# A Perceiver layer on one core: small tensor work of cross attention in two groups instead of three, and a new order of opening, loads and stores

## The chip, the cores and the metric

The kernel runs on one core of a Trainium2 chip. TensorE (PE) multiplies matrices, VectorE (DVE), ScalarE (ACT) and GpSimd (POOL) do elementwise work, and each engine works off its own queue of instructions in order. Transfers are issued from a queue too: nearly all of them here from SyncE's (SP). The metric is the device time of one execution in microseconds. Three executions of the kernel before are given, with their median; one more was taken with the hardware profiler.

## The reference

One layer of a Perceiver block with 16 batches: 64 latents of 512 numbers attend to 512 context rows of 512 numbers and to themselves (8 heads of 64), then the 1,024 latent rows attend to each other within a batch by differential self attention, then a gated feed-forward net follows whose weights and inputs are rounded to a 4-bit float format in blocks of 16. Cut to what matters, for each batch:

```python
# cross attention; g_*, b_* are layer norm vectors
latents = layer_norm(x)
xn, ln = layer_norm(ctx, g_x, b_x), layer_norm(latents, g_l, b_l)
q      = ln @ w_q                             # 64 x 512, 8 heads of 64
k, v   = split(concat([xn, ln]) @ w_kv, 2)    # 576 x 512 each
sim    = q @ k.T * 64**-0.5                   # masked by the context mask
x      = x + layer_norm(softmax(sim) @ v @ w_out, g_o, b_o)
# self attention: two softmax maps a head, their difference weighs v, then Wo
x      = x + diff_attention(layer_norm(x), Wq, Wk, Wv, Wo)
# feed forward: fp4 rounds to the 4-bit grid, a scale for each block of 16
z      = fp4(layer_norm(x))
h      = silu(z @ fp4(w_gate).T) * (z @ fp4(w_up).T)
x      = x + fp4(h) @ fp4(w_down).T
```

## The kernel before

Everything is worked in fp32r products of split numbers: each operand is a high part (a cast) and a low part (the rest, a subtraction), and a product is three passes, high by high, low by high and high by low (`terms`, line 121). A product of a 128x512 result is so 12 matmuls of 128x128 weights by 128x512 data. The first three parts of the kernel run in the order of the program on every engine: `in_order` chains each engine's instructions. A few lines decide everything that the change moves.

The opening (`_latents`) loads the latents, normalises them (`moments`, `norm`), transposes tiles by TensorE (`turn`) and splits them into `lnh` and `lnl` (`halves`, lines 527 and 528). `high` and `low` (lines 479 and 483) split the weights into `wkh`, `wkl` and so on. `heads(g, what, …)` makes the latents' keys (`lk`) and queries (`lq`), tile by tile, and after each step of a product it calls what `during(step, …)` had hung there: 40 steps in all, which carry the splits of the other weights and the first batches' context. Four batches of latents make a group of 256 columns.

Cross attention loops over 16 batches. In each, four tiles of keys (`keys(b, m)`, 12 large matmuls into `pk`, evicted by DVE at line 804) and four tiles of values (`values(b, t)`, into `pv`, evicted by ACT at line 817) are worked. Between them lie three groups of small tensor work:

- after keys 1: the transposes of the previous batch's second half of probabilities (`turn_both`, `prt`, 8 matmuls) and of its latent columns (`turn_latents`, `prlt`, 2 matmuls); in every second batch also a transpose of the output (`out_turn`)
- after keys 2: `finish(b - 1)`, that is 80 small weighing matmuls (`av`, line 898, tiles of 128x64), and `scores(b, 0)`: 16 matmuls (`sim`, line 830, tiles of 64x64), followed by `softmax` on DVE (line 849) and ACT (line 853)
- after values 1: `turn(b, 0, 0)` and `turn(b, 0, 1)` (8 transposes), `scores(b, 1)`, and in every second batch the output product (`out_product`, 12 large matmuls)

Around them are put, in the order of the program, the work for batches to come: `Context.load` (a 1 MB load of `nat` for the row statistics), `fetch` (256 KB of the transposed context each), `high` and `low` (the split of it), `stats` and `spread` and `flat` (the rows' scale, laid out by a DVE transpose and four small DMAs), `every` (the scale loaded again as a row), `begin` (mask, queries and `vl`, the latents' values: a memset on POOL and two loads) and `around` (the latents' keys, two small DMAs a tile). `weight_o` splits the output weights in batch 0. A `Quantise` object rounds 35 pieces of the feed-forward weights meanwhile: a call of `tick` advances every piece under way by one step and starts a new piece on each 4th tick (`EVERY`). A piece loads 256 KB, is rounded in several DVE, ACT steps, is transposed by DVE (`q_hl`, one buffer), split, and stored by a DMA at line 293. There are ten ticks in a batch (three in batch 0).

Memory for results: `ps_mm` has three banks (large products and transposes), `ps_sim` two pairs (scores, `turn_both`), `ps_av` one (weighing). The values `v` have four buffers.

Self attention (`SelfAttention.rest`) works eight tiles of 128 rows. The first two are worked at the end of `cross_attention`, together with the end of the last batch (`finish(B - 1)`, `out_norm(NT - 1)`, `att.end(1)`), and the weights' splits `att.split`. In `rest`, `norms` is a list of steps of the feed-forward's input norms, taken from by `parts`, a number of steps for each tile. The feed forward (`FeedForward`) is set by a scheduler with costs and due times; its input order on each engine does not depend on the change.

Of the kernel before, what the change touches and what calls it, by code (L numbers as in the profile page):

```python
# [240 lines left out]
class Quantise:  # L241
# [6 lines left out]
    EVERY = 4  # L248

    def __init__(self, cm, sc, i):  # L250
# [10 lines left out]
        self.clock, self.active = 0, []  # L261
# [4 lines left out]
    def tick(self, new=True):  # L266

        if new and self.jobs and self.clock % self.EVERY == 0:
            self.active.append(self.piece(*self.jobs.pop()))
        self.clock += 1  # L270
        self.active = [job for job in self.active if next(job, None)]
# [5 lines left out]
    def piece(self, which, c, k, src):  # L277
# [6 lines left out]
        yield from cm.fp4_steps(self.w1, w, n, name, True, True)  # L284
# [8 lines left out]
        nc.sync.dma_start(dst[:, :, k, :], f32(hl))  # L293


class Context:
# [38 lines left out]
    def flat(self, b):  # L335

        if b < B:
            cm, nc = self.cm, self.cm.nc
            nc.vector.transpose(cm.rsT, cm.rsw)
# [115 lines left out]
def _latents(ctx, tc, cm, sc, i, cw, cx, sa):  # L455
# [25 lines left out]
    def low(name, w, k):  # L481
        by = (nc.vector, nc.gpsimd)[k % 2]
        by.tensor_tensor(w[1][:, k, :], raws[name, k], f32(w[0][:, k, :]), ALU.subtract)
# [39 lines left out]
    def halves(p):  # L523
        g, n = divmod(p, GT)
        ln = rows.pop(p)
        hi, lo = (t[:, :, n * P : (n + 1) * P] for t in lns[g])
        nc.vector.tensor_copy(hi, ln)
        nc.vector.tensor_tensor(lo, ln, f32(hi), ALU.subtract)
# [60 lines left out]
    def heads(g, what, w, dst, scale, bias=None):  # L589
# [14 lines left out]
        made = []  # L604
        for m in range(KC):
# [8 lines left out]
            if m < late:  # L614
                next(terms)
                next(terms)
            if m < late - 1:
                continue
            for at, done, steps in made:
                for _ in steps:  # L620
                    pass
                then()
                take(at, done)
            made = []
        nc.sync.dma_start(dst[g], st)
# [16 lines left out]
    load(0)  # L642
    cw.load(pool)
    load(1)
# [5 lines left out]
    moments(1)  # L650
    cw.turn()
    norm(0)
    norm(1)
# [3 lines left out]
    halves(0)  # L657
    for k in range(1, KC):
        high("k", w_k, k)
    halves(1)  # L660
    for k in range(KC):
        low("k", w_k, k)
# [10 lines left out]
    during(3, bias_sum, "q", cw.bq, S**-0.5)  # L673
# [33 lines left out]
    during(19, cx.flat, 0)  # L707
    during(19, cx.load, 1)
    during(22, cx.every, 0)
    during(39, cx.spread, 1)  # L710
    during(39, cx.load, 2)
    for g, _ in enumerate(groups):
        heads(g, "k", w_k, sc.k, 1.0)
        heads(g, "q", w_q, sc.q, S**-0.5, cw.bq)
        if g + 1 < len(groups):
            for p in groups[g + 1]:
                turn(p)
                halves(p)
# [4 lines left out]
def cross_attention(tc, cm, sc, i, cw, cx, w1, w2, att, quant):  # L723
# [29 lines left out]
    def begin(b):  # L753
# [9 lines left out]
        vl = w2.tile([P, D], F32, tag="two_l", bufs=2, name=f"vl_{b}")  # L763

        nc.gpsimd.memset(vl, 0.0)
        for h in range(2):
# [5 lines left out]
        state[b] = dict(mu=mu, vl=vl, k=[], v=[], tot=cm.small.tile([P, KC], F32, tag="tot", name=f"tot_{b}"))  # L772
# [34 lines left out]
    def values(b, t):  # L807
# [8 lines left out]
        v = w1.tile([P, D], F32, tag="v", bufs=4, name=f"v_{b}_{t}")  # L816
# [51 lines left out]
    def turn_both(b):  # L868

        pt = cm.two(f"prt_{b}")  # L870
        for r in range(2):
            cm.transpose_chunks(pt[:, r, :], state[b]["pr", 1][:, r, columns_of(r)[1]], NJ)
        for r in range(2):
            turned(b, 1, r, pt[:, r, :])

    def turn_latents(b):
        st = state[b]
        prl = w2.tile([P, 2, P], F32, tag="two_h", bufs=2, name=f"prl_{b}")
        pt = cm.tr(f"prlt_{b}")[:, : 2 * P].rearrange("p (n q) -> p n q", q=P)
# [106 lines left out]
    for b in range(B):  # L986
# [12 lines left out]
        if b >= 4 and b % 2 == 0:  # L999
            out_moments((b - 4) // 2)  # L1000
        tick()
        keys(b, 1)
        cx.low(b + 1, 0)
        cx.high(b + 1, 1)
        tick()
        if b:
            turn_both(b - 1)
            turn_latents(b - 1)
        if done is not None:
            out_turn(done)  # L1010
        keys(b, 2)
# [7 lines left out]
        if b:  # L1019
            finish(b - 1)  # L1020
# [3 lines left out]
        scores(b, 0)  # L1024
        softmax(b, 0)
        around(b + 1, 2, 3)
        keys(b, 3)
        cx.fetch(b + 2, 1)
        cx.low(b + 1, 2)
        cx.high(b + 1, 3)  # L1030
        tick()
        values(b, 0)
        cx.every(b + 1)
        cx.low(b + 1, 3)
        cx.stats(b + 2, 0)
        tick()
# [3 lines left out]
        if b == 0:  # L1040
            load_o(0)
            load_o(1)
        values(b, 1)
# [3 lines left out]
        tick()  # L1047
        if b == 0:
# [648 lines left out]
```

## Time and profile before

| what | us |
|---|---|
| median of 3 executions | 925.25 (924.92 to 925.33) |
| profiled execution | 924.27 |
| its span (first to last instruction) | 922.5 |
| what lies around the span | 1.77 |
| granted TensorE clock, mean | 1.000 |
| opening until TensorE runs steadily | 16.0 |
| latents, keys and values of them | 75.6 (16.0 to 91.6) |
| cross attention, batches 0 and 1 | 41.8 (91.6 to 133.4) |
| cross attention, batches 2 to 15 | 426.6 (133.4 to 560.0) |
| end of cross attention and self attention | 153.0 (560.0 to 713.0) |
| feed forward | 209.5 (713.0 to 922.5) |

In a row of the profile `L121` is line 121 of the kernel before (of the kernel after, in rows of that one); PE is TensorE's matmuls and PEld its weight loads, which overlap. `out<-in` are the program's names of tiles. In a row of a timeline the first number is the start, the second the length of the run of instructions that is put together on the row, and `[0.88 <-DMA mask<-q_d]` says that the engine was idle for 0.88 us before and what ended the wait. A row with `x12` starts with the first of 12 instructions; the starts of successive rows give the pitch. The large matmuls of cross attention (128x512) follow each other at a pitch of 0.227 us, so the 12 of a product take 2.72.

### The profile page before, as it was taken

To read this page: it belongs to the slowest core of one execution; us is meant where nothing else is said; L and a number is where in the kernel's file an instruction comes from. 1 tells how busy PE (TensorE), PEld (TensorE's weight loads), DVE (VectorE), ACT (ScalarE), POOL (GpSimd) and SP (SyncE) were. 2 spreads that over 40 slices of the span, in tenths; PEclk is the share of its full clock that TensorE was granted. 3 is DMA by queue.
4 is the path that set the end of the run, shared out by engine and by line. 5 is a ranking of instruction groups with operands and counts; after the bars stand their busy time and mean duration, and the time that the engine had idled before them with its cause. 6 is when DMAs were issued, how large, how long until landed. Compare 5 with 4: busy or idle time off the path is not lost.

```text
span 922.5 us, 17526 instructions
## 1 busy us (share of the span) xinstructions
PE 897.4 (97%) x6774; PEld 741.2 (80%) x6774; DVE 683.2 (74%) x1384; ACT 392.3 (43%) x750; POOL 328.4 (36%) x378
## 2 busy tenths in 40 slices
PE   4999999999999999999999999999999999999998
PEld 4998778778877887887878877777888788888886
DVE  6545457878799787786987864575888698888875
ACT  4465255544545444444444445444344333323221
POOL 3245143326344363263443622556474321100000
PEclk9999999999999999999999999999999999999999
DMA  6464556454555455345544351140005630000000
GB/s 232 180 222 145 161 149 189 137 182 145 162 142 162 152 163 170 111 141 146 168 137 150 122 177 70 47 183 1 2 1 201 234 137 12 12 12 12 12 12 23
DMA packets 80234, 111.11 MB, mean 120 GB/s; under 512 B 33160, under 2 KB 38808, under 8 KB 78872
## 3 DMA queue, kind: packets, MB, share of 16 engines
q1 hardware_dynamic: 79992, 109.48, 36.9%
q8 instruction: 53, 0.87, 0.4%
q0 software_dynamic: 160, 0.52, 0.2%
q14 instruction: 29, 0.24, 0.1%
HBM read 84.26 MB, written 25.72 MB: 119 GB/s over the span
## 4 chain that ended last, share of the span: by engine, by line
PE 84%; DVE 7%; ACT 3%; POOL 2%; DMA 2%; SPq 1%; issue 1%; ACTq 0%; DVEq 0%; POOLq 0%
PE pv L121 18%; PE pk L121 18%; PE gu L121 13%; PE dn L121 7%; PE av L898 4%; PE sim L830 4%; PE prt L171 3%; PE lk L121 3%; PE lq L121 3%; PE lv L121 2%; PE po L121 2%; PE wo L121 2%; DVE ex L1239 1%; PE Wv L121 1%; PE ht L171 1%
## 5 line engine op out<-in xcount | busy, mean ns | idle before, releaser
L121 PE MATMUL pv<-xvh,x 128*128 128x512 f32 x512 | 133.4, 392 | 1.1 <-ACT prT L865 1.1
L121 PE MATMUL pk<-x,xkh 128*128 128x512 f32 x512 | 130.4, 397 | 0.0
L121 PEld LDWEIGHTS pv<-xvh,x 128*128 128x128 f32 x512 | 95.2, 188 | 24.7 <-issue 2.6
L121 PEld LDWEIGHTS pk<-x,xkh 128*128 128x128 f32 x512 | 93.7, 188 | 25.4 <-issue 3.9
L817 ACT ACTIVATE v<-pv,rs 128x512 f32<-128x512 f32 x64 | 43.9, 686 | 78.8 <-PE pv L121 78.7
L804 DVE TENSOR_TENSOR k<-pk,row 128x512 f32<-128x512 f32 x64 | 43.7, 684 | 45.1 <-PE pk L121 45.1
L368 POOL TENSOR_TENSOR x<-raw,x 128x512 fp32r<-128x512 f32 x32 | 44.2, 1383 | 79.4 <-ACT x L362 79.4
L853 ACT ACTIVATE pr<-pr,least 128x576 f32<-128x576 f32 x64 | 49.2, 772 | 52.4 <-DVE least L849 52.1
L121 PE MATMUL pk<-x,xkl 128*128 128x512 f32 x256 | 68.6, 390 | 0.0
L121 PE MATMUL pv<-xvl,x 128*128 128x512 f32 x256 | 68.5, 389 | 0.0
L121 PE MATMUL gu<-uT,fx 128*128 128x512 f32 (+1 forms) x288 | 67.2, 377 | 0.0
L121 PE MATMUL gu<-gT,fx 128*128 128x512 f32 (+1 forms) x288 | 65.5, 375 | 1.1 <-DVE h L1533 0.6
L121 PEld LDWEIGHTS gu<-gT,fx 128*128 128x128 f32 x288 | 52.3, 188 | 9.0 <-ACT fx L129 0.9
L121 PEld LDWEIGHTS gu<-uT,fx 128*128 128x128 f32 x288 | 51.9, 188 | 7.3
L121 PEld LDWEIGHTS pk<-x,xkl 128*128 128x128 f32 x256 | 48.1, 188 | 10.3
L121 PEld LDWEIGHTS pv<-xvl,x 128*128 128x128 f32 x256 | 48.1, 188 | 10.2
L849 DVE CUSTOM_DVE_ANT_0 pr<-sim,mask 128x576 f32<-128x576 f32 x64 | 45.9, 755 | 9.9 <-PE sim L830 9.1
L121 PE MATMUL dn<-dT,hh 128*128 128x512 f32 x176 | 44.8, 394 | 0.6 <-ACT hh L129 0.6
L205 ACT ACTIVATE qe_h<-qe_h,mmagic 128x512 f32<-128x512 f32 (+1 forms) x24 | 16.5, 688 | 67.2 <-DVE qe_h L202 64.0
L321 DVE BATCH_NORM_STATS2 cst<-nat 128x6 f32<-128x512 f32 x64 | 42.8, 669 | 0.0
L865 ACT COPY prT<-prt 128x512 f32<-128x512 f32 x64 | 34.1, 585 | 18.0 <-PE prt L171 18.0
L898 PEld LDWEIGHTS av<-v,prT 128*64 128x64 f32 x1024 | 36.7, 138 | 5.6 <-issue 5.6
(303 smaller groups left out, 1972.7 us busy)
## 6 DMA issues: line engine op xcount, KB each, us to landing
nat<-in_ctx_dram SPq DMA_DIRECT2D x16, 1024.0 KB
raw<-in_ctxT_dram SPq DMA_DIRECT2D x64, 256.0 KB
d_d<-qhl_d SPq DMA_DIRECT2D x11, 512.0 KB
row<-rs_d SPq DMA_DIRECT2D x16, 256.0 KB
g_d<-qhl_g SPq DMA_DIRECT2D x8, 512.0 KB
u_d<-qhl_u SPq DMA_DIRECT2D x8, 512.0 KB
gT<-g_d SPq DMA_DIRECT2D x4, 1024.0 KB
uT<-u_d SPq DMA_DIRECT2D x4, 1024.0 KB
```

The lines of the kernel that those rows point to most:

```text
L121: self.nc.tensor.matmul(ps, lhsT=p[i], rhs=p[j], start=start and n == 0, stop=stop and n == last)
L171: self.nc.tensor.transpose(pt[:, c * P : (c + 1) * P], src[:, c * P : (c + 1) * P], self.ident)
L205: nc.scalar.activation(e, e, AF.Relu, bias=self.mmagic, scale=MAGIC)
L321: nc.vector.bn_stats(st, self.nat[b][:, j, :])
L368: by.tensor_tensor(lo, self.raw[:, c, :], f32(hi), ALU.subtract)
L804: nc.vector.tensor_tensor(k[:, S : S + N], ps, cx.row[b], ALU.mult)
L817: nc.scalar.mul(v, ps, cx.rs[b][:, t : t + 1])
L830: nc.tensor.matmul(pss[r][c * S : (c + 1) * S, h, :half], lhsT=queries[b % 2][rows, m, :], rhs=st["k"][m][rows, at : at + half], start=Tru ...
L849: nc.vector.tensor_tensor_reduce(two(pr), ps[:, :, :half], two(mask), -1.0, BIG, ALU.add, ALU.min, least)
L853: nc.scalar.activation(pr, pr, AF.Exp, bias=least, scale=-1.0, accum_out=st["tot"][:, t : t + 1])
L865: nc.scalar.copy(prT, pt.rearrange("p (j q) -> p j q", q=P))
L898: nc.tensor.matmul(st["av"][rows, 2 * a + r, :], lhsT=w[:, rows], rhs=v[:, at : at + S], start=(n == 0), stop=(n == len(pairs) - 1),)
```

## The change

- The opening: `load(0, 1)` loads both of the first latents tiles before the small vectors; `moments(1)` follows `norm(0)`; `halves` becomes `upper` (the casts) and `lower` (the subtractions), and the casts of both tiles come first; all four `wkl` are subtracted on DVE; the first three `lk` products go term by term (high by high for all three, and so on); the eviction of the first group's `lq` tiles lags two tiles behind; `bias_sum` of q moves from step 3 to step 5.
- The groups: scores(b, 0) move ahead to the group after keys 1, in which the transposes of the previous batch now use `ps_mm` and the latents' use `ps_av`; `finish(b - 1)`, the two transposes and scores(b, 1) make one group after values 0.
- Other work around them: `vl` is zeroed after the first group and loaded after values 2 (`latent_zero`, `latent_values`, split from `begin`); `cx.load(b + 2)` in the first group takes the place of `cx.load(b + 3)` at the end of a batch; the DMAs of `flat` become `send`, one product later; `around(b + 1, 2, 3)` and `out_moments` lie after values 0; the output weights' splits move to the end of batch 0 and into batch 1; `v` has five buffers.
- The quantiser: nine ticks a batch (five in batch 0); a piece begins each 3.6 ticks; two idle ticks in each piece; the stores are issued from ScalarE's queue.
- The end: `Wv`'s second half is split before `finish(B - 1)`, `out_norm(NT - 1)` comes before `att.end(1)`, and the norms in `rest` are taken in another order, with a third place for them after `end(n)`.

```diff
-    EVERY = 4
+    EVERY = 3.6
...
-        if new and self.jobs and self.clock % self.EVERY == 0:
+        if new and self.jobs and self.clock >= self.begun * self.EVERY:
+            self.begun += 1
...
-        yield from cm.fp4_steps(self.w1, w, n, name, True, True)
+        for step, _ in enumerate(cm.fp4_steps(self.w1, w, n, name, True, True)):
+            yield True
+            if step in (1, 4):
+                yield True
...
-        nc.sync.dma_start(dst[:, :, k, :], f32(hl))
+        nc.scalar.dma_start(dst[:, :, k, :], f32(hl))
...
-    def halves(p):
-        g, n = divmod(p, GT)
-        ln = rows.pop(p)
-        hi, lo = (t[:, :, n * P : (n + 1) * P] for t in lns[g])
-        nc.vector.tensor_copy(hi, ln)
-        nc.vector.tensor_tensor(lo, ln, f32(hi), ALU.subtract)
+    def upper(*tiles):
+        for p in tiles:
+            g, n = divmod(p, GT)
+            nc.vector.tensor_copy(lns[g][0][:, :, n * P : (n + 1) * P], rows[p])
+
+    def lower(*tiles):
+        for p in tiles:
+            g, n = divmod(p, GT)
+            hi, lo = (t[:, :, n * P : (n + 1) * P] for t in lns[g])
+            nc.vector.tensor_tensor(lo, rows.pop(p), f32(hi), ALU.subtract)
...
-            if m < late:
-                next(terms)
-                next(terms)
             if m < late - 1:
                 continue
-            for at, done, steps in made:
-                for _ in steps:
-                    pass
+            for _ in range(3):
+                for _, _, steps in made:
+                    next(steps)
+            for _ in made:
                 then()
-                take(at, done)
+            ready += made
             made = []
+            while len(ready) > lag:
+                take(*ready.pop(0)[:2])
...
-    halves(0)
     for k in range(1, KC):
         high("k", w_k, k)
-    halves(1)
+    upper(0, 1)
+    lower(0, 1)
     for k in range(KC):
-        low("k", w_k, k)
+        low("k", w_k, k, nc.vector)
...
         keys(b, 1)
+        if b == 1:
+            weight_o(2)
+            weight_o(3)
         cx.low(b + 1, 0)
         cx.high(b + 1, 1)
-        tick()
         if b:
-            turn_both(b - 1)
+            turn(b - 1, 1, 0)
+            turn(b - 1, 1, 1)
             turn_latents(b - 1)
+        cx.load(b + 2)
+        scores(b, 0)
         if done is not None:
             out_turn(done)
+        softmax(b, 0)
+        latent_zero(b)
+        tick()
         keys(b, 2)
...
-        if b:
-            finish(b - 1)
+        keys(b, 3)
+        cx.fetch(b + 2, 1)
+        cx.send(b + 1)
...
-        scores(b, 0)
-        softmax(b, 0)
-        around(b + 1, 2, 3)
-        keys(b, 3)
...
         values(b, 0)
         cx.every(b + 1)
+        around(b + 1, 2, 3)
         cx.low(b + 1, 3)
         cx.stats(b + 2, 0)
+        if b >= 4 and b % 2 == 0:
+            out_moments((b - 4) // 2)
...
+        if b:
+            finish(b - 1)
+        turn(b, 0, 0)
+        turn(b, 0, 1)
+        scores(b, 1)
+        softmax(b, 1)
+        if done is not None:
+            out_product(done)
+        quant.tick()
         values(b, 1)
...
-        turn(b, 0, 0)
-        turn(b, 0, 1)
-        scores(b, 1)
-        softmax(b, 1)
+        values(b, 2)
+        latent_values(b)
         around(b + 2, 0, 1)
...
-        cx.load(b + 3)
-    turn_both(B - 1)
+    turn(B - 1, 1, 0)
+    turn(B - 1, 1, 1)
     turn_latents(B - 1)
     att.product(0, "Wq")
     att.split("Wv", 0, 1)
+    att.split("Wv", 2, 3)
     finish(B - 1)
     att.rope(0, "Wq")
-    att.split("Wv", 2, 3)
...
+    out_norm(NT - 1)
     att.end(1)
-    out_norm(NT - 1)
...
-        norms = iter(first[:5] + second[:1] + first[5:] + second[1:])
+        norms = iter(first[:3] + second[:1] + first[3:4] + second[1:2] + first[4:] + second[2:])
-        parts = {3: (1, 1), 4: (1, 1), 5: (2, 2), 6: (2, 1), 7: (1, 2)}
+        parts = {3: (1, 0, 1), 4: (2, 1, 1), 5: (1, 1, 1), 6: (1, 1, 0), 7: (1, 1, 1)}
```

## The prediction

> **What bounds the kernel now.** I read the page first, then busy time by stage (the trace cut where the work changes kind), then TensorE's timeline for every gap in its row, then the other engines around those gaps.
>
> ```profile
> PE 897.4 (97%) x6774; PEld 741.2 (80%) x6774; DVE 683.2 (74%) x1384; ACT 392.3 (43%) x750; POOL 328.4 (36%) x378
> 0.00:16.00 16.00, 3.68 (x13) 2.54 (x13) 9.54 (x14) 7.60 (x14) 8.64 (x20) 1.00 0.71 246
> 16.00:91.60 75.60, 75.31 (x522) 70.27 (x523) 42.13 (x79) 38.74 (x87) 28.84 (x36) 1.00 0.52 183
> 91.60:133.40 41.80, 38.85 (x265) 30.32 (x263) 17.14 (x36) 16.64 (x32) 14.12 (x15) 1.00 0.59 173
> 133.40:560.00 426.60, 426.60 (x3275) 343.14 (x3276) 341.43 (x726) 202.20 (x406) 171.91 (x197) 1.00 0.50 151
> 560.00:713.00 153.00, 148.97 (x1662) 121.31 (x1654) 104.42 (x194) 67.06 (x113) 79.66 (x84) 1.00 0.18 67
> ```
>
> The rows after the first hold: window, its length, busy time of PE, PEld, DVE, ACT and POOL, granted clock, DMA share, GB/s. TensorE is the bound at 97%. Of the 25.1 us in which it is idle, 12.3 lie in the opening, 2.95 in batches 0 and 1 (91.6 to 133.4), none in batches 2 to 15, 4.0 in self attention. So a gain is to be had from named gaps, or from TensorE's own work, and there only from how it is grouped: no matmul is removed.
>
> **The opening: -2.0.**
>
> ```profile
> 9.94 2.67 POOL L483 TENSOR_TENSOR wkl<-raw_k,wkh 128x512 fp32r<-128x512 f32 x2 [2.51 <-ACT wkh L479]
> 10.41 1.08 DVE L527 CAST lnh<-ln 128x512 fp32r<-128x512 f32 x1
> 11.52 1.64 DVE L528 TENSOR_TENSOR lnl<-ln,lnh 128x512 fp32r<-128x512 f32 x1
> 13.08 1.48 DVE L527 CAST lnh<-ln 128x512 fp32r<-128x512 f32 x1
> 14.71 1.20 PE L121 MATMUL lk<-lnh,wkh 128*128 128x256 f32 x4 [5.70 <-DVE lnh L527]
> 16.29 1.23 PE L121 MATMUL lk<-lnl,wkh 128*128 128x256 f32 x4 [0.39 <-DVE lnl L528]
> 21.48 0.64 PE L121 MATMUL lk<-lnh,wkh 128*128 128x256 f32 x4
> 31.81 0.43 DVE L527 CAST lnh<-ln 128x512 fp32r<-128x512 f32 x1 [2.17 <-ACT ln L520]
> ```
>
> A cast beside POOL's subtraction takes 1.08 and 1.48, without it 0.43 (31.81). The change puts both casts ahead of the low parts and takes the wkl off POOL, so lnh is whole at about 11.7 (ln of tile 1 ends at 10.5, a cast of 0.43 to 0.6 each), not 14.6. That is not a gain of 2.9: next come both lnl (0.69 to 1.64 each, to about 13.5 to 15) and all four wkl on DVE at 0.64 each (the row of two in the trace took 1.28), so to about 16 to 17.6. Three lk tiles are worked term by term; their 36 matmuls end 0.48 a four (0.85 until 19.05) after the last wkl, and lk_3 begins at about 19.5 in place of 21.48. All later steps are PE-bound (75.31 of 75.6), so it carries through: -2.0, bounds -1.2 and -3.0. Loading x before the small vectors brings tile 0 and 1 earlier by some tenths and is within these. The sum of bq (during 3 to 5) and the lag of the lq evictions only move work away from the first q tiles; cover is the 0.82 a q tile leaves; without it 0.8.
>
> **Batches 0 and 1: -0.5 -1.24 -1.15.**
>
> ```profile
> 100.80 2.23 PE L830 MATMUL sim<-k,mask 64*64 64x288 f32 x16 [0.88 <-DMA mask<-q_d]
> 117.45 1.19 PE L121 MATMUL pv<-xvh,x 128*128 128x512 f32 x4 [1.08 <-ACT prT L865]
> 131.26 0.34 PE L898 MATMUL av<-vl,prl 128*64 128x64 f32 x4 [0.99 <-ACT prl L883]
> ```
>
> The last two stalls, 1.08 and 0.99, are copies queued on ACT behind other work (weight_o, the prl copy) while PE wants their result or bank; with the switch after each (0.16) they cost 1.24 and 1.15. After the change weight_o lies behind values 2 of batch 0 and keys 1 of batch 1, out of the way of the first, and prl has 36 large matmuls (8.4 us) until its use instead of 12: both go. What they would become if ACT is later still: the same stalls, so bounds 0 and -2.4. The first stall (0.88 and a slow first part, 2.23 for 1.13) is different: in batch 0 the scores move 2.7 us forward, behind keys 1. What is late next is key 1 (1.1 us after its last matmul) and the batch's twelve small key DMAs on SP, 0.6 each from 96.2. Against it, the 1 MB of nat and vl's memset and DMAs no longer stand ahead of them. I take -0.5, bounds +1.5 and -1.0.
>
> **The three groups made two: +0.4.**
>
> ```profile
> 217.32 1.03 PE L171 MATMUL prt<-ident,pr 128*128 128x128 f32 x8
> 218.32 2.09 PE L121 MATMUL pk<-x,xkh 128*128 128x512 f32 x8
> 223.73 1.20 PE L830 MATMUL sim<-k,mask 64*64 64x288 f32 x16
> 224.86 2.11 PE L121 MATMUL pk<-x,xkh 128*128 128x512 f32 x8
> 233.18 1.03 PE L171 MATMUL prt<-ident,pr 128*128 128x128 f32 x8
> 234.14 1.20 PE L830 MATMUL sim<-k,mask 64*64 64x288 f32 x16
> 235.27 1.20 PE L121 MATMUL pv<-xvh,x 128*128 128x512 f32 x4
> ```
>
> Starts in this row give prices of each passage. Twelve large matmuls are 2.72 alone. Before, G1 is 1.00 (ten prt), 12 large with one switch 2.93, G2 2.48 + 1.13, 24 large 5.6, G3 0.97 + 1.13. A large run behind sim loses 0.15 (235.27 to 236.31: 1.04, not 0.91), behind prt 0.12, prt to sim costs 0.18 more than prt to large. A batch without out product is 28.98 in the row. In the new order: 10 prt 1.19 + sim 1.13 + 36 large 8.40 + weighing 2.48 + 8 prt 0.97 + sim 1.13 + 60 large 13.745 = 29.045, +0.06; with out work 32.135 for 32.145. Over 15 batches +0.4. The reason: the number of passages from large to small falls by one, but sim (64x64 tiles) is now entered twice from a 128x128 transpose and so a passage between small ones takes its place. The Trainium skill, "TensorEngine Tiling (Array Packing)", section "Key Properties", has the rule that speaks against the change: changing the tiling mode, not just the tile, drains TensorE. By the rule the modes change six times a batch (128, 64, 128 | 128x64, 128, 64, 128) where they changed five; at the row's 0.1 to 0.2 a change that is +1.5 to +3, an estimate. "One group fewer at 0.2" would be -3. The row's sum lies between, and I take it: +0.4, bounds -1.8 and +1.5.
>
> **Keys, quantiser and stores: +1.0.** scores(b,0) now reads k_1 some 1.4 us after its last matmul starts (ten transposes and the switch); the eviction on DVE (0.69) ends 1.12 after it when DVE is free: 0.3 of slack, and in 5 of 15 batches it ended at +1.29 to +1.97. In the new order nothing stands between k_0 and k_1 on DVE, and ticks are fewer (140 for 153). The stores go to ACT's queue: in odd batches one stands behind the eviction of v_2, so it starts later; DVE's next transpose of a piece writes the one qhl buffer and waits until the store has landed, with 3.5 us of DVE work queued behind it, so k_0 and k_1 can be late by 0 to 0.8 in seven batches. Value +1.0, bounds 0 and +5. The issuing costs ACT 35 x 0.57 = 20 us; ACT is busy 202 of 427 us here, so nothing; without that cover prT and v would be late by 0.57. On SP they go missing, to its good; it was never the last. The 1 MB nat is issued after the batch's small DMAs in both orders (182.8 for a first use at 199.9: 17 us); vl's DMAs move past values 2 but are used a batch's half later; the fifth v buffer costs no time; weight_o, out_moments and send are covered by batches 1 and 2 (PE without a gap), 0.7 of DVE each if not.
>
> **Self attention: -1.2.**
>
> ```profile
> 617.33 0.81 DVE L155 TENSOR_SCALAR oz<-po,mv_o 128x512 f32<-128x512 f32 x1
> 618.79 0.66 PE L171 MATMUL ot<-ident,on 128*128 128x128 f32 x4 [0.77 <-DVE on L1311]
> 642.75 0.81 ACT L166 ACTIVATE fz<-x,mv_f 128x512 f32<-128x512 f32 x1 [2.86 <-POOL mv_f L160]
> 644.09 0.66 PE L171 MATMUL zt<-ident,z 128*128 128x128 f32 x4 [0.86 <-ACT qT L1209]
> 659.80 1.15 PE L1275 MATMUL wt<-ident,w 64*64 64x64 f32 x32 [0.32 <-DVE x L1339]
> ```
>
> out_norm ahead of end(1) takes oz from in front of L1311: -0.65. The later fz takes 0.81 from in front of qT: -0.86. Wv's halves split ahead of the last weighing: -0.5 (its wait of 0.52 on POOL). But at the fourth tile a norm's statistics (0.69 + 0.18) now stand in front of L1339, where PE already waits 0.32: +0.88. Small rest -0.1. Sum -1.23; with each of the gaps kept or closed alone, bounds +0.9 and -2.1. The feed-forward stage keeps its order: 0.
>
> **Sum.** -2.0 - 0.5 - 1.24 - 1.15 + 0.4 + 1.0 - 1.23 = -4.7. The profiled execution took 924.27 us, span 922.5 and 1.77 around it; it becomes 919.6. The median of the runs is 0.98 above it, so 920.5.
>
> **Rivals.**
> (a) Late keys and the drains at their bounds: stores and late keys cost +4 in place of +1.0, the groups +1.5 in place of +0.4: 4.1 more, 924.6. For it: DVE is busy 341 of 427 us, and the slack is 0.3. Against: the thinner ticks. This case straddles "same".
> (b) The opening gains 3.0, the stores cost nothing, batch 0 gains 1.0, and the groups save 1.0: 3.9 less than the sum, 916.6. For it: casts of 0.43 are seen. Against: DVE's chain of six subtractions comes next.
> (c) Slower: DVE lags behind at keys 1 of every batch, because scores(b,0) no longer has 12 large matmuls (2.7 us) between it and the eviction. At the lateness seen once (batch 6, +1.97, 0.55 beyond the slack) in 15 batches it is +8.3: 928.8. It decides from 0.44 of stall a batch on (6.6 over 15, to pass 927.1). Against: 10 of 15 are on time with more ticks.
> (d) The regrouping does not do what it says (passages saved): that is my likeliest case already.
>
> **How the numbers follow.** The likeliest case (gain of 2.5 to 6.5) has 0.68 and gives 920.5; (a) 0.14, (b) 0.10, (c) 0.08. About 0.2%, 1.85 us, is what a measurement of this kernel can tell from no change. Faster: 0.68 + 0.10 + 0.06 of (a) = 0.84; same 0.08, the rest of (a); slower 0.08. The range of 916.2 to 924.6 leaves out (c), half of (a) and a third of (b), under 2 in 10.
>
> **What would show it.** Right: lk_3 at about 19.5; no gap before pv at batch 0's values and before av with prl; a batch without out product of 29.0 between the same matmuls; self attention's gaps before ot and zt gone, and one of about 1.2 before wt in the fourth tile. Wrong: gaps before sim released by k (L804 before, some lines on after); batches over 29.3 or under 28.85; lk_3 later than 20.3.

## The result and the profile after

The kernel after takes 922.57 us (median of 7 runs, 921.43 to 922.83); the kernel before took 925.25 in the same comparison (7 runs, 924.32 to 926.38). The ratio is 0.9968, 95% interval 0.9957 to 0.998. That is 2.7 us less, inside the forecast range and on the forecast side, but 4.7 less were forecast. The profiled execution took 922.76 us, its span 921.0.

From the page of the kernel after, the busy times, and two DMA queues (packets, MB, share of the engines' time). The second queue holds the stores that ScalarE now issues:

```profile
PE 898.7 (98%) x6774; PEld 740.6 (80%) x6774; DVE 682.9 (74%) x1386; ACT 396.2 (43%) x750; POOL 327.7 (36%) x376
q1 hardware_dynamic: 70472, 92.18, 30.7%
q10 hardware_dynamic: 9520, 17.30, 5.1%
```

The totals say almost nothing: the same matmuls, 1.3 us more of busy PE. The stages say more. Each length below is the difference between the starts of two matmuls in TensorE's timeline (first `pk` of batch 0, first `pk` of batch 2, first `Wq`, first `gu`):

| stage, us | before | after | difference |
|---|---|---|---|
| opening and latents, to batch 0 | 91.59 | 89.49 | -2.10 |
| batches 0 and 1 | 58.91 | 55.43 | -3.48 |
| batches 2 to 15 | 430.51 | 435.43 | +4.92 |
| end and self attention | 132.36 | 131.46 | -0.90 |
| feed forward, to the end | 209.11 | 209.18 | +0.07 |

The table ahead of the prediction draws its borders elsewhere: by the first `pk`, batch 2 starts at 150.50 and batch 15 ends at 581.01, so its 133.4 lies within batch 1 and its 560.0 within batch 15. The differences add up to 1.5 us and not to 2.7, since each column is one execution, and the profiled one of the kernel before was 1.0 faster than its median.

So 6.5 us were gained in three places, and 4.9 given back in the one stage in which the profile had shown no idle time of TensorE. There it now waits. TensorE's timeline of the kernel after, all rows of batches 2 to 15 that show an idle time (shorter waits, or a wait spread over the matmuls of a row, do not show as one):

```profile
213.54 0.66 PE L171 MATMUL prt<-ident,pr 128*128 128x128 f32 x4 [1.26 <-DVE k L825]
275.66 0.66 PE L171 MATMUL prt<-ident,pr 128*128 128x128 f32 x4 [0.31 <-DVE k L825]
305.40 0.66 PE L171 MATMUL prt<-ident,pr 128*128 128x128 f32 x4 [0.44 <-DVE k L825]
551.84 0.66 PE L171 MATMUL prt<-ident,pr 128*128 128x128 f32 x4 [0.45 <-DVE k L825]
576.45 1.20 PE L121 MATMUL pv<-xvh,x 128*128 128x512 f32 x4 [0.34 <-ACT v L838]
```

Each of the first four is the second block of transposes in the first group: it wants the product bank that key 0 is evicted from. A batch undisturbed is seen here, with the new order of groups; the starts give 29.11 us a batch without output work and 32.21 with it, where the kernel before had 28.98 and 32.16 to 32.39:

```profile
150.36 1.03 PE L171 MATMUL prt<-ident,pr 128*128 128x128 f32 x8
151.23 0.38 PE L895 MATMUL prlt<-ident,pr 128*128 128x128 f32 x2
151.54 1.20 PE L851 MATMUL sim<-k,mask 64*64 64x288 f32 x16
152.67 2.14 PE L121 MATMUL pk<-x,xkh 128*128 128x512 f32 x8
163.58 1.09 PE L171 MATMUL prt<-ident,pr 128*128 128x128 f32 x8
164.60 1.20 PE L851 MATMUL sim<-k,mask 64*64 64x288 f32 x16
165.74 1.20 PE L121 MATMUL pv<-xvh,x 128*128 128x512 f32 x4
```

Why key 0 is late in the first of those gaps is read from the timelines of ScalarE, GpSimd and VectorE, in order of time (start, length, engine; ACTq is ScalarE's issue of a DMA; GpSimd's row is needed for run e1 below):

```profile
203.71 0.69 ACT L838 ACTIVATE v<-pv,rs 128x512 f32<-128x512 f32 x1 [0.82 <-PE pv L121]
203.77 0.52 ACTq L297 DMA_DIRECT2D u_d<-qhl_u  x1
207.39 1.29 POOL L968 TENSOR_TENSOR oz<-oz,g_o 128x512 f32<-128x512 f32 x1 [0.40 <-DVE oz L155]
208.43 0.71 DVE L291 STREAM_TRANSPOSE qhl_u<-qw_u 128x512 f32<-128x512 f32 x1 [1.12 <-DMA u_d<-qhl_u]
209.07 1.27 DVE L202 TENSOR_SCALAR qe_u<-qw_u 128x512 uint32<-128x512 uint32 x1
210.25 0.67 DVE L194 TENSOR_REDUCE qm_g<-qw_g 128x32 f32<-128x512 f32 x1
212.81 1.27 DVE L825 TENSOR_TENSOR k<-pk,row 128x512 f32<-128x512 f32 x2
```

The store's low part was ready at 202.74 (VectorE's row at 202.08, 0.66 long), but the store stands behind the eviction of v on ScalarE's queue, which waits for its product, and is issued at 203.77. The next piece's transpose writes the one `qhl` buffer, so it waits until the store has landed, at 208.43. Behind it, 4.4 us of VectorE's work stand before the two key evictions: key 0 ends 4.75 us after its last matmul started, where 1.12 is the time of a punctual one. By the profile VectorE waits 13 times for a store in this kernel, 33.7 us together, and not once in the kernel before.

How late key 0 may be can be read from the batches. In a batch undisturbed, the second block of transposes starts 3.4 us after key 0's last matmul did. Six of the batches 2 to 14 are longer than an undisturbed one, and each by what key 0 takes beyond 3.3 us; in the other seven key 0 ends after 2.94 at most, and nothing is lost:

| batch | 4 | 5 | 6 | 7 | 12 | 13 |
|---|---|---|---|---|---|---|
| key 0 ends after its last matmul's start, us | 4.75 | 3.60 | 3.81 | 3.93 | 3.52 | 3.56 |
| the batch is longer by, us | 1.46 | 0.29 | 0.50 | 0.66 | 0.23 | 0.26 |

These are 3.4 of the 4.9 us.

### The profile page after: what moved, and what is told of

It reads as the page before. It is cut to its first block, busy times and chain, and to the rows that moved or that the text cites. A ratio compares the mean times of both kernels' runs of the same rounds, so it can differ in the third digit from the quotient of the medians.

```text
span 921.0 us, 17499 instructions
## 1 busy us (share of the span) xinstructions
PE 898.7 (98%) x6774; PEld 740.6 (80%) x6774; DVE 682.9 (74%) x1386; ACT 396.2 (43%) x750; POOL 327.7 (36%) x376
## 4 chain that ended last, share of the span: by engine, by line
PE 77%; DVE 14%; DMA 4%; ACT 2%; issue 1%; POOL 1%; SPq 1%; DVEq 0%; ACTq 0%; POOLq 0%
PE pk L121 16%; PE pv L121 14%; PE gu L121 13%; PE dn L121 7%; PE sim L851 3%; PE av L911 3%; PE prt L171 3%; PE lv L121 2%; DMA u_d<-qhl_u 2%; PE po L121 2%; PE lq L121 2%; PE lk L121 2%; PE wo L121 2%; PE Wv L121 2%; DMA d_d<-qhl_d 1%
```

## The experiments

The theory (A) is that the store's place on ScalarE's queue made the loss of batches 2 to 15. The rival (B) is that the two groups themselves make the keys late, whatever the stores do; a third (C) that TensorE loses time in changing its tile shapes. Lengths of stages from the profiled execution of each run:

| kernel | median, us | to batch 0 | batches 0, 1 | batches 2 to 15 | self attention |
|---|---|---|---|---|---|
| before | 925.25 | 91.59 | 58.91 | 430.51 | 132.36 |
| after | 922.57 | 89.49 | 55.43 | 435.43 | 131.46 |
| e1: after, stores on SyncE | 919.10 | 89.75 | 55.43 | 431.82 | 131.45 |
| e2: before, stores on ScalarE | 926.41 | 92.53 | 59.49 | 431.33 | 132.40 |
| e3: before, new opening | 923.42 | 89.99 | 59.55 | 430.70 | 132.37 |
| e4: before, two groups | 950.23 | 91.86 | 62.42 | 452.96 | 132.31 |
| e5: e4, ticks behind the group | 941.73 | 92.20 | 60.75 | 445.92 | 132.37 |
| e6: e1, without idle ticks | 925.00 | 89.56 | 55.42 | 437.69 | 131.42 |
| e7: e1, output weights' old places | 919.70 | 89.47 | 55.56 | 432.19 | 131.38 |
| e8: e1, old end | 919.97 | 89.36 | 55.60 | 431.81 | 132.27 |
| e9: e1, three groups | 924.10 | 89.98 | 54.46 | 436.96 | 131.46 |
| e10: e1, old loads | 934.71 | 89.48 | 61.71 | 440.90 | 131.44 |
| e11: e1, two more edits | 917.99 | 89.29 | 55.60 | 431.82 | 130.30 |
| e12: e11, three groups, a tick moved | 916.75 | 89.78 | 55.56 | 430.24 | 130.63 |

**e1, stores back on SyncE's queue.**

```diff
-        nc.scalar.dma_start(dst[:, :, k, :], f32(hl))
+        nc.sync.dma_start(dst[:, :, k, :], f32(hl))
```

> The changed kernel with one edit: the 35 stores of the quantiser go back to SyncE's queue. Theory A (the stores behind the value evictions on ScalarE's queue land late, VectorE's next transpose waits for them, and the keys behind it come late): VectorE's 13 waits for a store (33 us together in the changed kernel) go, no gap of TensorE before prt is released by a key, and batches 2 to 15 take 3 to 4 us less, so about 919.5. Theory B (the keys come late because of the new order of groups and ticks, whatever queue stores): the gaps before prt stay at 2 to 2.5 us and the time at 922.5. A third outcome, SyncE's queue is blocked by the stores and loads come late: new gaps with a DMA as releaser, 923 or more.

919.1 us (918.95 to 919.37, 4 runs), ratio to before 0.9931 (0.9916 to 0.9946): 3.5 less than the kernel after from this line alone. Batches 2 to 15 take 3.6 less, and no row before `prt` shows an idle time. Theory A holds for the time, but its detail was too strong: by the profile VectorE still waits 12 times for a store, 15.8 us together instead of 33.7. It is the shorter wait, not none, that lets the keys come in time. At the same place as above, in VectorE's and SyncE's timelines:

```profile
202.60 0.57 SPq L297 DMA_DIRECT2D u_d<-qhl_u  x1
207.78 0.71 DVE L291 STREAM_TRANSPOSE qhl_u<-qw_u 128x512 f32<-128x512 f32 x1 [1.43 <-POOL oz L968]
```

In this run all is 0.3 us later than in the kernel after, so the store is issued 1.4 us earlier in the batch and the transpose runs 0.9 earlier. It still waits for the store: the view names GpSimd's `oz`, which ends at 207.72, but in the kernel after the same transpose starts in the middle of that step (208.43, where `oz` runs from 207.39 to 208.68) and so does not need it, and the trace counts the store's landing complete at 207.69. With the waits that the view puts down to this step, there are 15 in the kernel after, 36.5 us together, and 13 here, 17.3. Between the end of their low part and their issue the 35 stores stood 22.7 us together in the kernel after, and 7.7 here; from issue to landing they took 134.4 and 125.1. So the earlier issue is the larger part of the gain.

**e2, the converse on the kernel before.** The same line of the kernel before, SyncE to ScalarE.

> The kernel before with one edit: its stores are issued from ScalarE's queue. Theory A: VectorE waits for stores here too, keys come late (k_0 over 2 us after its last matmul), but the old first group has two banks of its own for the transposes, so that the time grows by less than in the changed kernel, 0 to 2 us: 925.3 to 927.5. Theory B: no change in the key times, 925.3.

926.41 us (925.07 to 927.85, 12 runs), ratio 1.0009 (1.0 to 1.0018). The bound of the time held, the mechanism did not: VectorE waits for a store once (1.25 us), and key 0 comes at 1.12 in 12 of 16 batches (14 in the kernel before). So the queue is no harm by itself, nor is a late issue: the stores of the kernel before stand 85.8 us together ahead of their issue on SyncE's queue, up to 7.05, and here 41.8 on ScalarE's. It hurts where VectorE is soon ready for the next transpose. From the end of a low part to that moment it is 6.9 us or more in the kernel before (median 8.9), in the kernel after 5.0 in the median, and in 13 of 34 cases under 4.6. What brings them so close, the pace of the quantiser, the places of its ticks or the groups, was not separated. The 0.9 us that this run's opening took longer is no part of the edit, which does not touch it; it shows how far openings of one and the same code lie apart.

**e3, the new opening alone.** `_latents` of the kernel after in the kernel before, with its load of context 2 left at step 39.

> The kernel before with the new opening alone (loads, casts first, low parts on VectorE, three products term by term, the lag, the sum of bq). If the stages add up, the first key product of cross attention starts 2.1 us earlier as in the changed kernel (91.6 to 89.5) and the time is 923.2. If the early start is given back at the first wait for a DMA in batch 0 (the sim gap of 0.88), 924.5 or more.

923.42 us (922.7 to 923.98, 8 runs), ratio 0.9976 (0.9966 to 0.9986): -2.0, as the stages add up. In the profiled execution 1.6 are gained up to batch 0, and 0.6 of it are given back in batches 0 and 1, so both expectations are partly seen; one execution is too few to say more.

**e4, the two groups alone.** The regrouping without the quantiser's pace, the new loads, the opening and the end:

```diff
-            turn_both(b - 1)
+            turn(b - 1, 1, 0)
+            turn(b - 1, 1, 1)
             turn_latents(b - 1)
+        scores(b, 0)
...
         values(b, 0)
...
+        if b:
+            finish(b - 1)
+        turn(b, 0, 0)
+        turn(b, 0, 1)
+        scores(b, 1)
```

> The kernel before with the two groups alone: scores(b,0) with the transposes after keys 1, finish, transposes and scores(b,1) after values 0, transposes in the banks of the products, latents' transposes in the weighing bank, five value buffers, around for tiles 2 and 3 after values 0. Ticks, stores, loads and opening are those of before. By the sum of the record (+0.4 for the tile modes, stalls of batches 0 and 1 gone or changed) 924 to 926. Theory B (the new groups make keys late on their own): gaps before prt or sim released by keys, 928 or more. A drain of 0.2 saved in each batch would give 922.

950.23 us (950.03 to 952.41, 4 runs), ratio 1.0272 (1.0257 to 1.0287): 25 us slower, far beyond what theory B asked for. Two kinds of gaps alternate. In a batch with output work, ScalarE's and TensorE's timelines:

```profile
191.78 0.72 ACT L205 ACTIVATE qe_u<-qe_u,mmagic 128x512 f32<-128x512 f32 x1 [2.94 <-DVE qe_u L202]
192.41 1.05 ACT L865 COPY prT<-prt 128x512 f32<-128x512 f32 x2
193.03 2.11 PE L121 MATMUL pk<-x,xkh 128*128 128x512 f32 x8 [1.22 <-ACT prT L865]
```

A quantiser's step on ScalarE waits 2.94 for VectorE, and the copies that free TensorE's banks stand behind it. In a batch without output work, VectorE's timeline and the gap that follows:

```profile
223.14 0.69 DVE L145 BATCH_NORM_STATS2 st_a<-x 128x6 f32<-128x512 f32 x1 [0.58 <-POOL x L957]
223.97 0.66 DVE L207 SCALAR_TENSOR_TENSOR qw_u<-qe_u,qw_u 128x512 f32<-128x512 f32 x1
224.66 0.69 DVE L208 SCALAR_TENSOR_TENSOR qw_u<-qw_u,qe_u 128x512 f32<-128x512 f32 x1
225.27 0.68 DVE L804 TENSOR_TENSOR k<-pk,row 128x512 f32<-128x512 f32 x1
226.00 1.29 PE L830 MATMUL sim<-k,mask 64*64 64x288 f32 x14 [1.62 <-DVE k L804]
```

The statistics of `out_moments` and two steps of a tick stand between key 0 and key 1 (the rows run from 223.14 to 225.27), and the scores, which now come right behind, wait for key 1. This is what the slower rival of the prediction described. Against an undisturbed batch with two groups, the six even batches from 4 to 14 are 13.4 us longer together and the six odd ones from 3 to 13 8.2; batch 0 takes 4.6 more than in the kernel before, its scores waiting 4.0 for the queries.

**e5, e4 with these two taken away.** The ticks after keys 0 and keys 1 follow the first group's softmax, and `out_moments` follows values 0.

> The kernel with the two groups alone (950.2 us), with the two ticks after keys 0 and keys 1 moved behind the first group's softmax, and out_moments moved behind values 0; nothing else of the change. If the loss of 25 us comes from what stands between k_0 and k_1 on VectorE (even batches, gaps before sim of 0.8 to 1.7) and from the quantiser's step ahead of the prT copies on ScalarE (odd batches, gaps of 1.22), these gaps go and the time is 925 to 930. If the two groups make keys late whatever the ticks, 940 or more.

941.73 us (940.09 to 944.29, 4 runs). The two kinds of gaps are gone, and only 8.5 of the 25 us with them: the wait moved. In batch 5:

```profile
266.91 0.71 DVE L287 STREAM_TRANSPOSE qhl_g<-qw_g 128x512 f32<-128x512 f32 x1 [1.84 <-DMA g_d<-qhl_g]
267.70 0.62 ACT L288 CAST qhl_g<-qhl_g 128x512 fp32r<-128x512 f32 x1 [6.58 <-DVE qhl_g L287]
268.22 0.68 ACT L817 ACTIVATE v<-pv,rs 128x512 f32<-128x512 f32 x1
268.96 1.41 PE L121 MATMUL po<-woh,oh 128*128 128x512 f32 x4 [3.08 <-ACT v L817]
```

VectorE's transpose waits for the previous store, ScalarE's cast of it waits 6.58 us for the transpose, the eviction of v stands behind the cast, and TensorE wants its bank. By the number this is the outcome that was to speak for theory B. By the chain it is the quantiser's steps that hold the engines, and not the groups alone; but at the same pace with three groups (the kernel before) no transpose waits for a store, so it takes both, the groups and the ticks at places that do not suit them. Batch 0 still waits 3.57 for its queries.

**e6, the pace.** e1 with the two idle ticks of each piece taken out.

```diff
-        for step, _ in enumerate(cm.fp4_steps(self.w1, w, n, name, True, True)):
-            yield True
-            if step in (1, 4):
-                yield True
+        yield from cm.fp4_steps(self.w1, w, n, name, True, True)
```

> The changed kernel with stores on SyncE's queue (919.1 us) and without the two idle ticks in each piece (nine ticks from load to store as before, pieces still begun each 3.6 ticks). If the thinning matters, keys are late in more batches and the time grows by 1 to 5 us; if only the places of the ticks matter, 919 within 0.7.

925.0 us (924.85 to 925.43, 12 runs), 5.9 more than e1, just above the upper end of what was expected. The two idle ticks add no work and no wait; they only change which step falls at which place of a batch. Without them key 0 ends 4.6 to 5.8 us after its last matmul started in batches 4, 6, 12 and 14, and each of these shows a gap before `prt`. A store is not needed for it: VectorE waits for stores only 3 times, 4.7 us together, and in batch 4, below, key 0 ends at 4.59, behind steps of two pieces.

```profile
213.44 0.66 PE L171 MATMUL prt<-ident,pr 128*128 128x128 f32 x4 [1.10 <-DVE k L822]
```

**e7, the output weights' splits at their old places** (in e1).

> The changed kernel with stores on SyncE's queue (919.1 us) and the output weights' splits where they were (0 and 1 after values 1 of batch 0, 2 and 3 after values 2). If these splits on ScalarE's queue made the two stalls of batches 0 and 1 (2.4 us with their switches), the time grows by up to 2.4, to 921.5; if the new groups take the stalls away whatever the order (the transposes now come before the splits), 919.

919.7 us (919.42 to 920.66, 4 runs), 0.6 more than e1, of which the profile shows 0.13 in batches 0 and 1 (55.56 for 55.43). The stalls before `pv` and before `av` that the prediction laid to these splits stay away with the splits at their old places, and with the old groups too (e9), so either of the two edits is enough.

**e8, the old end** (in e1).

> The changed kernel with stores on SyncE's queue (919.1 us) and the old end: Wv's second half split after the last weighing, out_norm after end(1), norms and their places as before. The prediction's sum for these is -1.23, so about 920.3; the profiles of before and after differ by 0.9 over that stretch, so 920.0.

919.97 us (919.92 to 920.14, 4 runs): 0.87 more than e1, 0.82 in the profile's stage. As expected from the profiles.

**e9, the three groups of before in e1.** Everything else of the change stays.

> The changed kernel with stores on SyncE's queue (919.1 us), but with the three groups of before (turn_both in its own pair of banks, scores(b,0) and finish after keys 2, transposes and scores(b,1) after values 1); thinned quantiser, loads, opening and end stay those of the change. If the new groups are worth nothing in TensorE's time (28.98 and 32.16 to 32.35 a batch before, 29.11 and 32.21 after) and the rest of the change makes the gain: 918 to 920. If the groups themselves gain, 922 or more.

924.1 us (922.75 to 924.92, 20 runs), 5.0 more than e1, so by its words the groups gain. But the profile shows another thing: the seven batches 2, 4, ... 14 without output work take 28.98, batch 0 takes 25.35 (26.31 in e1), and the loss lies in five batches with output work, at one place:

```profile
196.11 0.71 DVE L291 STREAM_TRANSPOSE qhl_u<-qw_u 128x512 f32<-128x512 f32 x1 [2.79 <-DMA u_d<-qhl_u]
196.90 0.62 ACT L292 CAST qhl_u<-qhl_u 128x512 fp32r<-128x512 f32 x1 [3.48 <-DVE qhl_u L291]
198.04 0.67 ACT L838 ACTIVATE v<-pv,rs 128x512 f32<-128x512 f32 x1
198.77 1.20 PE L121 MATMUL po<-woh,oh 128*128 128x512 f32 x4 [1.41 <-ACT v L838]
```

It is the chain of e5: a store, a transpose, a cast, an eviction, a bank. The ticks had been left where they suit the two groups.

**e10, the old loads** (in e1): `vl` zeroed and loaded in `begin`, the context load at its old places.

> The changed kernel with stores on SyncE's queue (919.1 us), with vl zeroed and loaded in begin, and the 1 MB context load for two batches on at the old places (step 39 of the opening, end of each batch). If the order on SyncE's queue ahead of batch 0's queries is what keeps its scores from waiting (the kernels with groups alone wait 3.6 to 4.0 us for the queries there), batch 0 takes 4 to 5 us more: 923 to 924. If the queries are early anyway, 919 to 920.

934.71 us (933.46 to 935.46, 4 runs), 15.6 more than e1. Batch 0 takes 6.3 more, the first row below being a part of it; 9.1 more lie in the later batches, which nobody had expected. The chain there, from POOL's, SyncE's, VectorE's and TensorE's timelines:

```profile
99.02 1.46 PE L860 MATMUL sim<-k,mask 64*64 64x288 f32 x5 [3.94 <-DMA mask<-q_d]
205.56 0.19 POOL L148 TENSOR_SCALAR mv_o<-mv_o 128x1 f32<-128x1 f32 x1 [5.49 <-DVE mv_o L146]
206.33 0.53 POOL L780 MEMSET vl<- 128x512 f32 x1
206.89 1.27 SPq L786 DMA_DIRECT2D vl<-v_d  x2
212.01 0.56 SPq L297 DMA_DIRECT2D u_d<-qhl_u  x1
216.16 0.71 DVE L291 STREAM_TRANSPOSE qhl_u<-qw_u 128x512 f32<-128x512 f32 x1 [3.80 <-DMA u_d<-qhl_u]
220.01 0.66 PE L171 MATMUL prt<-ident,pr 128*128 128x128 f32 x4 [1.46 <-DVE k L834]
```

The memset stands on POOL behind a step that waits 5.49 for VectorE; the loads of `vl` wait for the memset on SyncE's queue from 203.4 (the end of the issue before) to 206.89; the store stands behind them and is issued at 212.01, 0.5 us ahead of batch 4, where in e1 it was 3.9 ahead of it. The rest is theory A's chain with another cause for the late store. The run moves `vl` and the context load together; the chain shows the part of `vl`, and that of the context load was not separated.

**e11, two further edits on e1.**

```diff
-        during(2 + k, low, "v", w_v, k)
+        during(4 + k, low, "v", w_v, k)
...
-        parts = {3: (1, 0, 1), 4: (2, 1, 1), 5: (1, 1, 1), 6: (1, 1, 0), 7: (1, 1, 1)}
+        parts = {3: (1, 0, 1), 4: (1, 2, 1), 5: (1, 1, 1), 6: (0, 2, 0), 7: (1, 1, 1)}
```

> The changed kernel with stores on SyncE's queue (919.1 us) and two more edits: in self attention the statistics of the second tile come behind line 1356's sum at the fourth tile, and the first step of its rounding at the sixth (parts 4: (1, 2, 1), 6: (0, 2, 0)), which should take the gaps of 1.06 and 0.32 before wt to 0.25 and 0: -1.1; and in the opening the low parts of w_v come two steps later, behind the norms of tiles 2 and 3, which should take 0.4 to 1.0 before the transposes lt. Together 917.1 to 917.7; if the edits only move the waits to what follows (lv waiting for its low weights, a late rounding step), 919.

917.99 us (917.92 to 918.36, 5 runs), ratio 0.9921 (0.9907 to 0.9934). Self attention gains 1.15, as expected. The opening's edit gained little, at most the 0.2 to 0.5 by which openings differ anyway: e1 shows one wait before `lt`, of 0.41, and here there is one of 1.30.

```profile
27.73 0.63 PE L171 MATMUL lt<-ident,lz 128*128 128x128 f32 x4 [1.30 <-DVE lz L155]
653.02 1.15 PE L1292 MATMUL wt<-ident,w 64*64 64x64 f32 x32 [0.31 <-DVE x L1356]
```

**e12, the three groups with one tick moved,** on e11.

```diff
-        quant.tick()
         values(b, 1)
...
             out_product(done)
+        quant.tick()
         values(b, 2)
```

> The kernel of run e11 (918.0 us) with the three groups of before, and the tick that stands ahead of values 1 put behind the output product. In the run with the old groups (924.1) every batch without output work took 28.98 and batch 0 took 25.35, less than with the new groups (29.11 and 26.31), but five batches waited 1.2 to 1.8 for an eviction of values that stood on ScalarE's queue behind a quantiser's cast. If those waits come from the tick's place alone they go: 915 to 916, and the three groups are no worse than the two. If the store's landing makes them wherever the tick stands, they come elsewhere: 919 or more.

916.75 us (916.11 to 917.13, 4 runs), ratio 0.9908 (0.9891 to 0.9924). The five waits are gone; batches 2 to 15 take 430.24, 1.6 less than e11, and two small gaps in batch 1 (0.48 before `pk`, 0.28 before `av`) and one in batch 6 (0.36) keep it from the 915 to 916 expected. It beats both kernels of the case. Its interval overlaps that of e11, which was run against other runs of before, so it is not shown that three groups are faster than two; it is shown that they are no slower, once the ticks suit them; the moved tick stands where it stood in the kernel before. Late keys hurt less here: key 0 ends 2.3 to 4.6 us after its last matmul started in 13 batches, and only those with 4.51 and 4.64 show a gap for a key, as the transposes have a pair of banks of their own.

## Why the prediction was right, and where it was not

The time lies in the range and on the right side, 2.1 us above the likeliest value. The gains came where they were forecast, and one loss, that of the keys, was three times too small. Two terms came out right by errors that cancel, which is luck: the opening and the groups. And signs that the prediction itself had named as wrong were seen: three batches without output work are over 29.3 (30.57, 29.61 and 29.34), and batch 0 has a gap of 0.23 before `sim` for key 1.

- **The opening, -2.0:** measured -2.10 in the profile, -2.0 in e3, but not by the steps told. The first product began at 11.67, as forecast (11.7). The low parts and the weights' low parts on VectorE then ran undisturbed, the four `wkl` in 2.49, and lk_3 began at 17.62 and not at 19.5, 3.9 earlier than before, where the bound was 3.0; in the ten runs with the new opening it began at 17.6 to 19.2. The surplus was lost at what was late next, which the prediction did not ask: the norms of tiles 2 and 3, behind the bias sums, so that `lv` begins at 28.1 to 28.8 in all ten, whatever lk_3 did.

```profile
17.62 0.64 PE L121 MATMUL lk<-lnh,wkh 128*128 128x256 f32 x4
17.82 4.15 DVE L549 SCALAR_TENSOR_TENSOR ws_bq<-raw_q,vec,ws_bq 128x512 f32<-128x512 f32 x3
26.61 0.63 PE L171 MATMUL lt<-ident,lz 128*128 128x128 f32 x4 [0.31 <-DVE lz L155]
27.88 0.63 PE L171 MATMUL lt<-ident,lz 128*128 128x128 f32 x4 [0.64 <-DVE lz L155]
```

- **Batches 0 and 1, -2.9 together:** measured -3.48 (-2.42 and -1.06). Both stalls went. Their cause was too narrow: e7 puts the splits back and they stay away. The -0.5 for batch 0's queries has the right sign for the reason named, the loads ahead of them, and was too small: 2.42 less the 1.24 of its other stall leaves 1.2. e10 shows how much hung on it, a wait of 3.94 for them and 6.3 us of batch 0.
- **The groups, +0.4:** right in size by two errors that cancel. An undisturbed batch costs 0.13 more without output work (29.11 for 28.98) and 0.05 with it (32.21 for the 32.16 of batch 9), 1.2 for batches 2 to 14, where the prediction's 0.06 and -0.01 make 0.4. The sum had no price for the way from the weighing back to the transposes: the eight `prt` of the second group take 1.02 (163.58 to 164.60), and took 0.96 before (233.18 to 234.14). Against it, five batches with output work had waited 0.2 us each for `prl` between weighing matmuls in the kernel before, which its rows do not show as idle, and this went. With two late keys of 0.22 each, e1 takes 0.64 more than before from the first `pk` of batch 2 to that of batch 15. No drain was saved. The rule on tile modes that the prediction names, put at 0.1 to 0.2 for the one change more in a batch, is nearer to the undisturbed batches than the sum that was preferred to it: 0.13 without output work, 0.05 with it. Theory C is thus worth about 1 us, and does not explain the loss. The regrouping gains nothing; e12 reaches the lowest time without it.
- **Keys, quantiser and stores, +1.0:** this is the term that was mis-sized. Late keys cost 4.0 us, 3.4 in batches 2 to 14 and 0.6 in the last; e1 puts the stores' share at 3.5 us of the median and 3.6 of the stage. The step that failed is that the keys "can be late by 0 to 0.8 in seven batches", and with it the slack of 0.3 for key 1. The first to wait is not the scores for key 1 but the second block of transposes, for key 0's bank; the prediction had followed the tiles that the scores read, and not the banks that the transposes now take from the products. And key 0 was late by more than 1 us over its 1.12 in 12 batches, odd and even, by up to 3.6 (batch 4), to which waits for stores added (1.13 and 1.12 ahead of batch 4's). The loss stayed at 4.0 only because key 0 had 3.3 us, a slack that the prediction had not worked out. Of the 4.9 us of the stage the stores are 3.6, two keys that are late in e1 too 0.4, the groups 0.2 and the last batch 0.7. The bounds of 0 to +5 were wide enough.
- **The thinner ticks** were told as a small relief, and e6 shows 5.9 us for the two idle ticks of a piece.
- **The last batch** was no step of the sum: 34.99 us for 33.67, of which the stores are 0.65 (34.34 in e1). The remaining 0.67 contains the gap of 0.34 before `pv`; with three groups (e9, e12) it is 33.67 again.
- **Self attention, -1.23:** measured -0.90, e8 0.87. The gaps before `ot` and `zt` that were named and the one of the half of Wv are gone, and the wait before `wt` in the fourth tile is there with 1.08 (about 1.2 forecast), by the statistics named. A new gap of 0.76 before `ot` two tiles later, which the old end does not have (e8), was no term of the sum; it is the last row:

```profile
655.97 0.64 DVE L145 BATCH_NORM_STATS2 st_f<-x 128x6 f32<-128x512 f32 x1
656.74 0.66 DVE L1356 TENSOR_TENSOR x<-wo,x 128x512 f32<-128x512 f32 x1
657.46 1.15 PE L1292 MATMUL wt<-ident,w 64*64 64x64 f32 x32 [1.08 <-DVE x L1356]
684.09 0.66 PE L171 MATMUL ot<-ident,on 128*128 128x128 f32 x4 [0.76 <-DVE on L1328]
```

- **The slower rival** did not come in the changed kernel, but e4 gives its price: 13.4 us in the six batches with its gaps before `sim` and `prt`, where 8.3 were worked out from one late key. The rest of the 25 us is that of ScalarE's queue (8.2) and of batch 0's queries.

What stays open: how much of e6's 5.9 us would come back by moving single steps, what brings a store and the next transpose so close in the changed kernel, and whether a second `qhl` buffer would free the transpose of the store altogether, which was not tried.

## What to carry to other kernels

When an engine works in program order, background work is not priced by its busy time but by what it waits for at the place where it stands: here the queue of the stores was worth 3.5 us, two idle ticks 5.9, the places of a few loads and a memset 15.6, at the same work. When a consumer is moved nearer to its producer, follow every buffer that the moved work takes, banks too, work out how late each may be (3.3 us for key 0 here), and list what stands between the two on each engine that hands them on. And test the named idea by itself and the rest without it: the regrouping alone lost 25 us, and everything but the regrouping and the stores' new queue, with e11's and e12's edits, gained 8.5.

## What had not been expected of the hardware

- Elementwise work of VectorE and GpSimd took longer where both ran at the same time. The prediction had read this from two casts, but did not ask what would run beside the work that GpSimd kept. Three rows of the bias sums (line 549) took 4.15 us, most of it beside GpSimd's `wql` and `wvl`, and 2.33 in the kernel before, with GpSimd idle (the row below); the two `wql` on GpSimd took 7.50 for 3.13. It was not even: the four `wkl` on VectorE, beside the same `wql`, took 0.62 each, as long as two had without GpSimd (1.28 for the two, from 16.16 before). Moving `wkl` to VectorE made that part faster and the next part slower.

```profile
19.08 2.33 DVE L537 SCALAR_TENSOR_TENSOR ws_bq<-raw_q,vec,ws_bq 128x512 f32<-128x512 f32 x3
```

- A store of 512 KB freed its buffer for the next piece 4.7 us after its issue began (203.77 to 208.43), in a stretch in which the DMA engines were busy 59% of the time.
